# Visits' pieces on four PSUM tiles, batch 1's projections and sorting earlier, and indirect transfers paced by block

## The chip, the cores and the metric

The kernel runs on one core of a Trainium2 chip, as one launch. The metric is the device time of that launch in microseconds (us). All arithmetic is in float32.

## What is computed

The input x is 2 x 256 x 56 x 56: two images, 256 channels, N = 3136 pixels. Two layers follow each other. The first is a non-local block without softmax, so its products can be folded into one 256 x 256 matrix for each image. The second is causal attention over the 3136 pixels as tokens (4 heads of 64), and a mixture of 8 experts of which each token takes its best two.

```python
# layer 0, for each image b; inv, shift are the folded batch norm
f  = einsum('bgdn,bgdm->bgnm', theta(x), phi(x)) / n
y  = einsum('bgnm,bgdm->bgdn', f, g(x))
x  = relu((w_out @ y + b_out) * inv + shift + x)
# layer 1, t = x as tokens, 2 x 3136 x 256
q, k, v = split(layernorm(t) @ W_attn)
t  = t + (softmax(causal(q @ k.T / 8)) @ v) @ W_proj
z  = layernorm(t)
p  = softmax(z @ gate_w + gate_b)          # 8 experts, the two largest kept
t  = t + sum over the two: p[e] * (gelu(z @ W1[e] + b1[e]) @ W2[e] + b2[e])
```

## The kernel before

**Layer 0** (`gram`, `fold`, `apply`) ends at about 92 us with the tokens in `ts[b]`, 128 tokens to a partition block, 25 blocks (`chunk`) to an image; each row has room for 8 gate values and some bookkeeping. Its means and deviations are there too.

**Attention** (`layer1`, `attend`) runs batch 0 and then batch 1. Queries go in 7 blocks of 448 (index i), heads in two pairs (hp), keys in blocks of 128 (j). A step is one (i, hp, j): `scores` makes a score tile (`psc`, two buffers of two PSUM banks each, L721), ACT takes its exponential into `st` (L729; five buffers), DVE multiplies the diagonal blocks by a mask (L731) and adds the tile to a sum (L743); three steps later `values` multiplies by v (L761). Two steps of this order stand in the text as "s" and "y": they alternate on TensorE. When a query block of a head pair has had its last score and TensorE is three steps further, `attend` calls `visit(i, hp)`, and then `sum_rows` (L785).

A **visit** is the place for other matmuls. `ahead` gives its pieces: projections of the next segment's queries and keys (L603), values (L618) and transposes of the normalised tokens (L589), of the next batch too. Every piece takes a PSUM tile from `bank` (pool `pm`, tag "m", two buffers of one bank), which ACT or DVE evicts. A visit also runs output projections.

**The queue.** Work off the main line lies in generators in a queue; each `yield True` is one unit done, `yield False` means that nothing can be done now, and `yield "pe"` that matmuls come next. `pull(n)` runs n units from the first generators that have any. `between` calls it before each attention step (before: `pull(2)` in every other step), `meanwhile` after each block of the expert stage. `products`, called in visits, runs a generator that stands at "pe". For each batch b the generator `tokens` runs in turn:

- `project_out` (L671): pairs of 128-token groups through the output projection, each evicted by an add on DVE (L676), then the layer norm's statistics (`stats`, L177 and L178). With batch 1 each pair is followed by three units.
- `dispatch` (from L1000): the sorting. Softmax of the gate values, the two best experts, ranks by a matmul (L1122), places in the table of slots. Then 25 token groups are normalised (L1355) and scattered twice each by an indirect transfer from GpSimd (L1363) into `x_slots` in DRAM.
- for batch 0, the loads of the experts' first weights and of the first two groups of blocks.

**The expert stage** (`experts`) goes over 102 blocks of 128 slots. Block n runs `hidden` (L1485, sixteen matmuls), the transposes of a later block (L1462) and `outputs` of an earlier one (L1504). The slots come in groups of three blocks, fetched by SP six blocks ahead (L1403, L1408) and for batch 1 added to a second table's rows where both batches share a block (L1439). Blocks from 42 on hold batch 1; `need(1)` in the fetch for block 42, at n = 36, finishes batch 1's scatters if they are not all sent. Weights of a block's expert are copied by DVE (L1473). Results of blocks below 57 are stored to `y_slots`, those from 42 on are scattered to `y_tokens` by GpSimd (L1525).

Once block 56 is written, `finish(0)` joins the queue: for each pair of token groups it gathers the two experts' rows from `y_slots` (L1679, four indirect transfers), DVE adds them with their weights (L1714), TensorE transposes (L1727) and SP stores the result. `finish(1)` does the same for batch 1 from `y_tokens`, with plain loads (L1699).

Inside attention and inside the expert stage the order on every engine is as written out by these loops; nothing reorders it.

Of the kernel before, what the change touches and what calls it, by code (L numbers as in the profile page):

```python
# [10 lines left out]
F32 = mybir.dt.float32  # L11
# [17 lines left out]
def conv_attn_moe_kernel(  # L29
# [52 lines left out]
    P = 128  # L82
    B, C, N = x.shape
# [9 lines left out]
    W = 448  # L93
# [418 lines left out]
    def layer1(nm, general):  # L512

        with ExitStack() as whole:
# [4 lines left out]
            bg = pool(whole, "bg", bufs=2)  # L519
            g1 = pool(whole, "g1", bufs=1)  # L520

            def bank(name, shape=(P, 512)):
                return pm.tile(list(shape), F32, tag="m", name=f"{name}_{nm}")

            def centre_gate(place):
# [135 lines left out]
            def project_out(b, qT, done):  # L661

                for first, m, k in pairs():
                    while done() < (first + m - 1) * P + k:
                        yield False
                    yield "pe"
                    for n in range(first, first + m):
                        o = n * P
                        ps = bank(f"pp_{b}_{n}")
                        for c in range(NH):  # L670
                            nc.tensor.matmul(  # L671
                                ps[:k, : C + E], qT[:, c, o : o + k], wpr[:, c, :],
                                start=(c == 0), stop=(c == NH - 1),
                            )
                        t = ts[b][:k, n, : C + E]
                        nc.vector.tensor_tensor(t, t, ps[:k, : C + E], ALU.add)  # L676
                        if b == 0:
                            nc.sync.dma_start(out=rest_d[:k, n], in_=t[:, :C])
                    stats(b, first, m, k, bg, f"o{nm}{b}")

                    for _ in range(3 if b else 1):
                        yield True

            def attend(
                b, qT, kT, v, fst, fs, psc, py, visit, between, clock, later, finished
# [145 lines left out]
                for n in range(len(steps) + LAG):  # L831
                    if BEHIND < n <= len(steps) + BEHIND and steps[n - 1 - BEHIND][4]:
                        i, hp = steps[n - 1 - BEHIND][:2]
                        visit(i, hp)
                        sum_rows(hp, i)
                    if n < len(steps):
                        i = steps[n][0]
                        between(i, ends[i] - n)
# [165 lines left out]
            def dispatch(b):  # L1004

                t = ts[b]
                tail = chunk(NCH - 1)
                ops = [0]

                def small_piece():  # L1010

# [7 lines left out]

                def op():  # L1020

                    ops[0] += 1
                    for _ in range(0 if b else 1 + ops[0] % 2):
                        yield True

                def small(name, last=E, dt=F32):
# [2 lines left out]
                def wide(ap):  # L1029
# [8 lines left out]
                    small(k, 1).rearrange("p t o -> p (t o)") for k in ("newton_x", "newton_y", "red")  # L1038
                )
                nc.vector.tensor_scalar(x, var, 1e-5, None, ALU.add)  # L1040
                nc.vector.tensor_scalar(
                    y.bitcast(I32), x.bitcast(I32), 1, None, ALU.arith_shift_right
                )
                nc.vector.tensor_scalar(
                    y.bitcast(I32), y.bitcast(I32), -1.0, float(0x5F3759DF), ALU.mult, ALU.add
                )
                yield from small_piece()
                for i in range(4):
                    to = var if i == 3 else y
                    nc.vector.tensor_tensor(z, y, y, ALU.mult)  # L1050
                    nc.vector.tensor_tensor(z, z, x, ALU.mult)
                    nc.vector.tensor_scalar(z, z, -0.5, 1.5, ALU.mult, ALU.add)
                    nc.vector.tensor_tensor(to, y, z, ALU.mult)
                    yield from op()
                    yield from small_piece()
# [294 lines left out]
                for n in range(NCH):  # L1350
                    kk = chunk(n)
                    xr = (scatter_rows[0] if b else bg).tile(
                        [P, width], F32, tag="xr", name=f"xr_{nm}{b}_{n}"
                    )
                    nc.vector.tensor_scalar(  # L1355
                        xr[:kk, :C], t[:kk, n, :C],
                        t[:kk, n, MEAN : MEAN + 1], t[:kk, n, RSTD : RSTD + 1],
                        ALU.subtract, ALU.mult,
                    )
                    if b:  # L1360
                        nc.vector.tensor_copy(xr[:kk, C:], t[:kk, n, C + E - 2 : SLOT + 1])  # L1361
                    for k in range(2):
                        s = nc.gpsimd.indirect_dma_start(  # L1363
                            out=xds[b],
                            out_offset=bass.IndirectOffsetOnAxis(ap=idxs[b][:kk, k, n : n + 1], axis=0),
                            in_=xr[:kk],
                            in_offset=None,
                            bounds_check=xds[b].shape[0] - 1,
                            oob_is_err=False,
                        )  # L1370
                        group = f"x_slots_{nm}{b}"
                        tc.declare_no_dep(s.ins, group=group, reason="different rows")
                        tc.add_to_no_dep_group(group, s.ins)
                        if b or k:
                            yield True
                    if b == 0:
                        yield False
                sent[b] = True

            def experts(w1s, w2s, b2s, ex, es, ps6, between, need, written, settle, decide):  # L1380
# [282 lines left out]
            def finish(b, oy, bufs):  # L1663
# [3 lines left out]
                def fetch(n, m, k):  # L1667
# [8 lines left out]
                    ahead.append((n, m, k, ys, rows))  # L1676
                    for c, y in enumerate(ys):
                        for a in range(m):
                            nc.gpsimd.indirect_dma_start(  # L1679
                                out=y[:k, a],  # L1680
                                out_offset=None,
                                in_=y_slots,
                                in_offset=bass.IndirectOffsetOnAxis(
                                    ap=idxs[b][:k, c, n + a : n + a + 1], axis=0
                                ),
                                bounds_check=MIXED * P - 1,
                                oob_is_err=False,
                            )
                            yield True
# [106 lines left out]
                judged.append(True)  # L1796


            queue, held = deque(), set()

            def advance(g):
                held.discard(g)
# [21 lines left out]

            def products():

                for g in list(queue):
                    if g in held:
                        advance(g)
                        return  # L1830

            projected, placed, ranked, sent = ([False] * B for _ in range(4))
            side, worked, scattered = deque(), [0], []
            first, early_rows, scatter_rows, judged = [], [], [], []
            last_pool, hots = [], []

# [82 lines left out]
            else:  # L1919
                fst = pool(att, "fst", bufs=5)  # L1920
                fs = pool(end, "fs", bufs=2, side="right")
                psc = pool(att, "psc", bufs=2, space=PSUM)
                py = pool(att, "py", bufs=1, space=PSUM)
                projections = [project_qkv(b, qT, kT, v, px) for b in range(B)]
                finished = [[0] * NH for b in range(B)]
# [35 lines left out]
                for piece in keys[2:] + vs(0) + xs(1):  # L1961
                    piece()
                for b in range(B):
                    queue.append(tokens(b, qT, lambda b=b: min(finished[b])))

                    def visit(i, hp):

                        now, then = ahead(b, i, hp)
                        for piece in now:
                            piece()  # L1970
                        for _ in range(2):
                            pull()
                            products()
                        for piece in then:
                            piece()

                    def between(i, left):
                        if b == B - 1 and i == NB - 1 and left < NH * NCH - 2:

                            now = load_w2(left < NCH - 4)  # L1980
# [31 lines left out]
            with ExitStack() as moe:  # L2012
# [35 lines left out]
                    queue.appendleft(finish(1, oy, 3))  # L2048

                def meanwhile():  # L2050
                    sorting = projected[1] and not sent[1]
                    pull(3 if sorting or worked[0] >= MIXED else 2, every=True)
                    if side and next(side[0], None) is None:
                        side.popleft()

                def settle():
                    while queue:
                        pull(every=True)

                def decide():  # L2060
# [181 lines left out]
```

## Time and profile before

| | |
|---|---|
| median of 3 runs | 1320.96 us (1318.52 to 1323.38) |
| the profiled execution | 1319.58 us |
| its span, first to last instruction | 1317.9 us |
| TensorE busy | 1266.8 us |
| DVE, ACT, GpSimd busy | 789.5, 614.4, 343.9 us |
| mean granted TensorE clock | 0.990 |
| layer 0 and the first projections | 0 to 105.3 us, TensorE busy 101.0 |
| attention | 105.3 to 863.1 us, TensorE busy 738.0 |
| expert stage and end | 863.1 to 1317.9 us, TensorE busy 427.7 |

The profile is one execution. The page has the busy time of each engine, the span in 40 slices, and groups of instructions by line. A timeline lists instructions in order, with the idle time ahead of each and what released it in brackets: `[1.08 <-issue]` is 1.08 us of idle time in which the engine waited for nothing that the profile records. Windows give the busy time of every engine in a stretch. Line numbers are those of the kernel before; PE is TensorE, POOL is GpSimd, SP issues transfers.

### The profile page before, as it was taken

How to read it: one execution, taken by the hardware profiler on the slowest of the kernel's cores; microseconds unless marked ns; L12 is line 12 of the kernel's file. 1: busy time of each engine (PE TensorE's matmuls, PEld its weight loads, DVE VectorE, ACT ScalarE, POOL GpSimd, SP SyncE). 2: the span in 40 equal slices, each digit the busy share in tenths (PEclk: the TensorE clock that was granted, in tenths of full speed). 3: DMA queues.
4: the chain of work that ended last, by engine and by line, in shares of the span. 5: the costliest groups of instructions: out<-in, count | busy, mean ns of one | idle time of the engine just before them, and what ended most of it. 6: DMA issues, size and time to landing. Idle time of an engine off the chain costs nothing.

```text
span 1317.9 us, 28546 instructions
## 1 busy us (share of the span) xinstructions
PE 1266.8 (96%) x10809; PEld 821.1 (62%) x10809; DVE 789.5 (60%) x1673; ACT 614.4 (47%) x1235; POOL 343.9 (26%) x319
## 2 busy tenths in 40 slices
PE   8999999999999999999998999999989999899997
PEld 7875545544444445444443444479978899798996
DVE  1673566666777745756876677754843443454554
ACT  0255555556566545565654456542422333244432
POOL 1113220000002223220026630000066212665560
PEclk9999999999999999999999999999989999899999
DMA  9994100000000001000002243322144343555554
GB/s 314 347 348 147 32 16 25 24 17 17 16 10 9 24 1 32 24 9 9 16 28 77 73 140 96 105 72 65 57 142 139 115 113 94 161 177 185 185 169 128
DMA packets 111075, 123.88 MB, mean 94 GB/s; under 512 B 19704, under 2 KB 100841, under 8 KB 110931
## 3 DMA queue, kind: packets, MB, share of 16 engines
q1 hardware_dynamic: 100130, 95.18, 23.6%
q0 software_dynamic: 9840, 25.67, 5.8%
q8 instruction: 89, 1.46, 0.5%
q10 hardware_dynamic: 960, 1.11, 0.2%
q14 instruction: 56, 0.45, 0.1%
HBM read 62.06 MB, written 61.05 MB: 93 GB/s over the span
## 4 chain that ended last, share of the span: by engine, by line
PE 88%; DVE 5%; issue 3%; ACT 2%; DMA 2%; POOL 0%; SPq 0%; another core or an unknown queue 0%; DVEq 0%; POOLq 0%; ACTq 0%
PE sc_f L721 19%; PE yp_f L761 19%; PE ht_f L1485 13%; PE yp_f L1504 13%; PE qk_f L603 7%; PE v_f L618 4%; PE cp L410 3%; PE pp_f L671 3%; PE tp_f L1462 2%; PE gram L317 2%; DVE acc_f L743 1%; PE sp_f L785 1%; ACT st_f L729 1%; PE yo_f L1727 1%; DMA out_dram<-ot_f 1%
## 5 line engine op out<-in xcount | busy, mean ns | idle before, releaser
L743 DVE TENSOR_TENSOR acc_f<-acc_f,st_f 128x896 f32<-128x896 f32 (+5 forms) x372 | 376.0, 1011 | 147.3 <-ACT st_f L729 128.3
L729 ACT ACTIVATE st_f<-sc_f 128x896 f32<-128x896 f32 (+5 forms) x400 | 330.3, 838 | 215.0 <-PE sc_f L721 193.1
L761 PE MATMUL yp_f<-st_f,v_f 64*64 64x448 f32 (+6 forms) x3184 | 337.9, 500 | 4.6 <-DVE st_f L731 3.1
L721 PE MATMUL sc_f<-qT_f,kT_f 64*64 64x448 f32 (+6 forms) x3184 | 336.3, 499 | 5.6 <-ACT st_f L729 3.8
L1494 ACT ACTIVATE g_f<-ht_f,b1b 128x128 f32<-128x128 f32 x408 | 116.9, 372 | 253.5 <-PE ht_f L1485 120.7
L721 PEld LDWEIGHTS sc_f<-qT_f,kT_f 64*64 64x64 f32 x3184 | 118.1, 133 | 160.9 <-issue 139.9
L761 PEld LDWEIGHTS yp_f<-st_f,v_f 64*64 64x64 f32 x3184 | 117.0, 133 | 158.2 <-issue 128.7
L1485 PE MATMUL ht_f<-xT_f,w_f 128*128 128x128 f32 x1632 | 205.3, 278 | 10.2 <-issue 7.3
L1485 PEld LDWEIGHTS ht_f<-xT_f,w_f 128*128 128x128 f32 x1632 | 199.8, 194 | 17.7 <-issue 12.8
L773 POOL TENSOR_TENSOR qT_f<-acc_f 128x448 f32<-128x448 f32 x28 | 31.9, 1140 | 492.6 <-ACT acc_f L772 492.6
L1363 POOL DMA_INDIRECT x_slots<-xr_f,idx x100 | 110.1, 1101 | 154.9 <-DVE xr_f L1361 104.9
L1473 DVE COPY w_f<-w1s_f 128x1024 f32 x102 | 72.4, 712 | 86.6 <-PE ht_f L1485 31.2
L574 POOL TENSOR_SCALAR xn_f<-t 128x256 f32<-128x256 f32 (+1 forms) x50 | 81.9, 1645 | 158.7 <-PE xp_f L589 69.7
L1525 POOL DMA_INDIRECT y_tokens<-ys_f,to_f x57 | 58.2, 1021 | 125.8 <-DVE ys_f L1514 101.4
L603 PE MATMUL qk_f<-px_f,wat 128*128 128x512 f32 (+2 forms) x224 | 89.9, 556 | 0.6 <-ACT px_f L595 0.6
L1514 DVE TENSOR_TENSOR ys_f<-yp_f,kT_f 128x128 f32<-128x128 f32 x102 | 29.5, 290 | 96.5 <-PE yp_f L1504 69.3
L603 PEld LDWEIGHTS qk_f<-px_f,wat 128*128 128x128 f32 x224 | 42.2, 197 | 45.8 <-issue 41.0
L1504 PE MATMUL yp_f<-px_f,g_f 128*128 x204 | 62.2, 386 | 1.4 <-PE tp_f L1462 1.3
L1504 PE MATMUL yp_f<-kT_f,g_f 128*128 x204 | 61.9, 385 | 0.7 <-issue 0.7
L1504 PE MATMUL yp_f<-w2s_f,g_f 128*128 x204 | 62.2, 386 | 0.0
L1504 PE MATMUL yp_f<-v_f,g_f 128*128 x204 | 62.1, 386 | 0.0
L731 DVE TENSOR_TENSOR st_f<-st_f,keep 128x256 f32<-128x256 f32 (+1 forms) x112 | 45.1, 402 | 28.0 <-ACT st_f L729 26.4
(285 smaller groups left out, 1221.8 us busy)
## 6 DMA issues: line engine op xcount, KB each, us to landing
x_slots<-fill SPq DMA_DIRECT2D x1, 8190.0 KB
xb_f<-x_slots SPq DMA_DIRECT2D x60, 130.0 KB
x_slots<-fill SPq DMA_DIRECT2D x1, 7296.0 KB
y_slots<-ys_f SPq DMA_DIRECT2D x57, 128.0 KB
kept<-t SPq DMA_DIRECT2D x2, 3200.0 KB
x<-in_x_dram SPq DMA_DIRECT2D x14, 448.0 KB
rb_f<-inverses SPq DMA_DIRECT2D x56, 112.0 KB
y_f<-y_tokens SPq DMA_DIRECT2D x23, 256.0 KB
```

The lines of the kernel that those rows point to most:

```text
L574: nc.gpsimd.tensor_scalar(xn[:k, a], ts[b][:k, n + a, :C], ts[b][:k, n + a, MEAN : MEAN + 1], ts[b][:k, n + a, RSTD : RSTD + 1], ALU.subtr ...
L603: nc.tensor.matmul(ps[:, :w], wat[:, c, d0 : d0 + P], px[:, s % 2, c, :w], start=(c == 0), stop=(c == NH - 1),)
L721: nc.tensor.matmul(ps[h : h + HS, a, c0:W], kT[hp][rows, j * P + h : j * P + h + HS], qT[rows, hp, q0 + c0 : q0 + W], start=True, stop=True,)
L729: nc.scalar.activation(st[:k, :, c0:], ps[:k, :, c0:W], AF.Exp, scale=SCALE)
L743: nc.vector.tensor_tensor(acc[:k, :, c0:], acc[:k, :, c0:], st[:k, :, c0:], ALU.add)
L761: nc.tensor.matmul(yp[a * HS : (a + 1) * HS, h // HS, c0:W], v[hp][h : h + HS, j, a, :HS], st[h : h + HS, a, c0:], start=first, stop=bool( ...
L1363: s = nc.gpsimd.indirect_dma_start(out=xds[b], out_offset=bass.IndirectOffsetOnAxis(ap=idxs[b][:kk, k, n : n + 1], axis=0), in_=xr[:kk], i ...
L1473: nc.vector.tensor_copy(w, w1s[:, :, bass.ds(e, 1), :].rearrange("p c e h -> p c (e h)"))
L1485: nc.tensor.matmul(ht[:, k, :], w[:, c, k * P : (k + 1) * P], xT[:, c, :], start=(c == 0), stop=(c == NH - 1),)
L1494: nc.scalar.activation(g[:, k, :], ht[:, k, :], AF.Gelu, bias=b1bs[b][:, k, i : i + 1])
L1504: nc.tensor.matmul(yp[:, :C], g[:, k, :], w2s[k][:, bass.ds(e, 1), :].rearrange("p e d -> p (e d)"), start=(k == 0), stop=(k == KH - 1),)
L1525: s = nc.gpsimd.indirect_dma_start(out=y_tokens, out_offset=bass.IndirectOffsetOnAxis(ap=to[:, n % GB : n % GB + 1], axis=0), in_=ys, in_o ...
```

## The change

- In a visit, `bank` counts its calls (`ring`) and gives tiles 1 and 2 from `pm` and tiles 3 and 4 from the score pool `psc`, and so on in turn. `visit` sets the count and clears it at its end, ahead of `sum_rows`.
- `project_out` no longer takes statistics on the spot. It puts a generator `closer` in the queue that does one group's statistics a unit: for batch 0 at the front, for batch 1 ahead of the queue's last entry. No unit follows a pair of batch 0 any more, and one follows a pair of batch 1. Only when all statistics of the batch are taken does it go on.
- `products` walks the batches, not the queue, and advances a batch's projections until it has done one pair. A visit calls it twice, now without a `pull` before each.
- `between` pulls one unit each step in place of two in every other step, and none in the cut (diagonal) steps of the first query block.
- `dispatch` for batch 0 yields after each operation, the Newton steps' too, where before it yielded once and twice in turn, and the four operations of a Newton step counted as one. In its scatter loop a unit follows each pair of transfers, and a second one that was a `yield False`.
- `finish(0)` issues one or two gathers a block in turn (`gathered`, `turn`). While batch 1's scatters go on `meanwhile` pulls two or three units in turn, in place of three; from block 57 on four in place of three.

```diff
             def bank(name, shape=(P, 512)):
+                turn = ring[0] % 4 if ring else 0
+                if turn > 1:
+                    ring[0] += 1
+                    flat = score_banks[0].tile([P, 2, 512], F32, tag="sc", name=f"{name}_{nm}")[:, 0]
+                    ...
+                    return flat[:, : shape[1]]
+                if ring:
+                    ring[0] += 1
                 return pm.tile(list(shape), F32, tag="m", name=f"{name}_{nm}")
...
-                    stats(b, first, m, k, bg, f"o{nm}{b}")
-
-                    for _ in range(3 if b else 1):
+                    if b == 0:
+                        queue.appendleft(closer(b, first, m, k))
+                    else:
+                        queue.insert(len(queue) - 1, closer(b, first, m, k))
                         yield True
+                while unclosed[b]:
+                    yield False
+
+            unclosed = [NCH] * B
+
+            def closer(b, first, m, k):
+
+                for n in range(first, first + m):
+                    stats(b, n, 1, k, bg, f"o{nm}{b}")
+                    unclosed[b] -= 1
+                    yield True
...
                 def op():
-                    ops[0] += 1
-                    for _ in range(0 if b else 1 + ops[0] % 2):
+                    if b == 0:
                         yield True
...
                     if b == 0:
-                        yield False
+                        yield True
                 sent[b] = True
...
                         for a in range(m):
+                            while gathered[0] == 1 + turn[0] % 2:
+                                yield False
+                            gathered[0] += 1
                             nc.gpsimd.indirect_dma_start(
...
             def products():
-                for g in list(queue):
-                    if g in held:
+                for b, g in enumerate(batches):
+                    if projected[b]:
+                        continue
+                    r = "pe" if g in held else advance(g)
+                    while r is True and not projected[b]:
+                        r = advance(g)
+                    if r == "pe":
                         advance(g)
                         return
...
                         now, then = ahead(b, i, hp)
+                        ring.append(0)
                         for piece in now:
                             piece()
                         for _ in range(2):
-                            pull()
                             products()
                         for piece in then:
                             piece()
+                        ring.clear()
-                    def between(i, left):
+                    def between(i, left, cut):
...
-                        if tick[0] % 2:
-                            pull(2)
+                        if not cut or i:
+                            pull()
...
                 def meanwhile():
-                    sorting = projected[1] and not sent[1]
-                    pull(3 if sorting or worked[0] >= MIXED else 2, every=True)
+                    gathered[0] = 0
+                    turn[0] += 1
+                    if placed[1] and not sent[1]:
+                        pull(2 + turn[0] % 2, every=True)
+                    else:
+                        pull(
+                            4 if worked[0] >= MIXED else 3 if projected[1] and not sent[1] else 2, every=True
+                        )
```

More of the change, by code (lines that the diff above doesn't have):

```diff
@@ L520, in layer1 @@
             g1 = pool(whole, "g1", bufs=1)
+            ring, score_banks = [], []
             def bank(name, shape=(P, 512)):
+                turn = ring[0] % 4 if ring else 0
+                if turn > 1:
+                    ring[0] += 1
+                    flat = score_banks[0].tile([P, 2, 512], F32, tag="sc", name=f"{name}_{nm}")[:, 0]
+                    if shape[2:]:
+                        return flat[:, : shape[1] * shape[2]].rearrange("p (a w) -> p a w", a=shape[1])
+                    return flat[:, : shape[1]]
+                if ring:
+                    ring[0] += 1
                 return pm.tile(list(shape), F32, tag="m", name=f"{name}_{nm}")
@@ L837, in attend @@
                         i = steps[n][0]
-                        between(i, ends[i] - n)
+                        between(i, ends[i] - n, (steps[n][2] + 1) * P > i * W + 1)
                     late = n >= LAG and steps[n - LAG][3]
@@ L1007, in dispatch @@
                 tail = chunk(NCH - 1)
-                ops = [0]
                 def small_piece():
@@ L1040, in dispatch @@
                 nc.vector.tensor_scalar(x, var, 1e-5, None, ALU.add)
+                yield from op()
                 nc.vector.tensor_scalar(
@@ L1043, in dispatch @@
                 )
+                yield from op()
                 nc.vector.tensor_scalar(
@@ L1046, in dispatch @@
                 )
+                yield from op()
                 yield from small_piece()
@@ L1050, in dispatch @@
                     nc.vector.tensor_tensor(z, y, y, ALU.mult)
+                    yield from op()
                     nc.vector.tensor_tensor(z, z, x, ALU.mult)
+                    yield from op()
                     nc.vector.tensor_scalar(z, z, -0.5, 1.5, ALU.mult, ALU.add)
+                    yield from op()
                     nc.vector.tensor_tensor(to, y, z, ALU.mult)
@@ L1796, in judge @@
                 judged.append(True)
-            queue, held = deque(), set()
+            queue, held, batches = deque(), set(), []
             def advance(g):
@@ L1833, in layer1 @@
             side, worked, scattered = deque(), [0], []
+            gathered, turn = [0], [0]
             first, early_rows, scatter_rows, judged = [], [], [], []
@@ L1922, in layer1 @@
                 psc = pool(att, "psc", bufs=2, space=PSUM)
+                score_banks.append(psc)
                 py = pool(att, "py", bufs=1, space=PSUM)
@@ L1963, in layer1 @@
                 for b in range(B):
-                    queue.append(tokens(b, qT, lambda b=b: min(finished[b])))
+                    batches.append(tokens(b, qT, lambda b=b: min(finished[b])))
+                    queue.append(batches[b])
                     def visit(i, hp):
                         now, then = ahead(b, i, hp)
+                        ring.append(0)
                         for piece in now:
@@ L2057, in settle @@
                     while queue:
+                        gathered[0] = 0
                         pull(every=True)
```

## The prediction

> **What bounds the kernel now.** I read the page first: busy shares, slices, instruction queue.
>
> ```profile
> PE 1266.8 (96%) x10809; PEld 821.1 (62%) x10809; DVE 789.5 (60%) x1673; ACT 614.4 (47%) x1235; POOL 343.9 (26%) x319
> ...
> PE   8999999999999999999998999999989999899997
> ...
> PEclk9999999999999999999999999999989999899999
> ...
> q8 instruction: 89, 1.46, 0.5%
> ```
>
> TensorE has work 96% of the span of 1317.9 us, so no edit here gains more than its idle time plus what it loses at a lowered clock. Idle is 51.1 us. Windows over the stages split it: 4.3 us before attention, 19.8 in attention (105.3 to 863.1), 18.9 from 863.1 until TensorE's last matmul, 8.2 behind that while the last output lands. The first and the last part are out of the change's reach; 38.7 us are within it. Then who ended TensorE's waits:
>
> ```profile
> PE ht_f L1485 <- issue: 7.3, 13, 1.1
> PE tp_f L1462 <- issue: 3.4, 4, 2.0
> PE yp_f L761 <- DVE st_f L731: 3.1, 7, 1.1
> ...
> PE xp_f L589 <- DVE t L676: 2.2, 6, 1.2
> PE sp_f L785 <- ACT kT_f L611: 1.8, 7, 0.4
> ```
>
> The columns are total us, times, longest. Two families: small waits for PSUM evictions around the visits, and "issue", where a matmul waited for nothing recorded. For the second I opened TensorE's timeline:
>
> ```profile
> 1133.51 1.05 PE L1485 MATMUL ht_f<-xT_f,w_f 128*128 128x128 f32 x8
> 1134.86 0.36 PE L1485 MATMUL ht_f<-xT_f,w_f 128*128 128x128 f32 x1 [0.30 <-issue]
> 1136.30 0.27 PE L1485 MATMUL ht_f<-xT_f,w_f 128*128 128x128 f32 x1 [1.08 <-issue]
> 1137.02 0.27 PE L1485 MATMUL ht_f<-xT_f,w_f 128*128 128x128 f32 x1 [0.45 <-issue]
> ...
> 1142.02 1.01 PE L1504 MATMUL yp_f<-px_f,g_f 128*128 x2 [0.85 <-PE tp_f L1462]
> ```
>
> Matmuls that run eight in 1.05 us suddenly come one by one, and at 1142 a pair takes 1.01 us instead of 0.59. The windows of that stretch give engines' busy time, clock, and DMA share and rate (last three columns):
>
> ```profile
> 1125.00:1130.00 5.00, 5.00 (x35) 4.66 (x33) 0.97 (x3) 1.63 (x7) 3.98 (x4) 1.00 0.79 249
> ...
> 1135.00:1140.00 5.00, 2.38 (x8) 1.64 (x9) 0.38 (x2) 0.00 (x0) 3.78 (x5) 0.73 0.50 161
> 1140.00:1145.00 5.00, 3.73 (x11) 2.74 (x10) 1.50 (x4) 2.60 (x10) 2.20 (x3) 0.50 0.20 60
> ```
>
> GpSimd (fifth) is 76 to 80% busy in the stretch's first two windows shown, issuing indirect transfers one behind the other. By the steady lengths in TensorE's timeline (hidden 1.78, transpose 0.22, output product 1.73: 3.73 us a block) I priced each such place, idle and lowered clock together: 974.0 to 987.2 holds 5.46 us of work, 7.7 lost; 1004 to 1009.8, 3.8; 1019.1 to 1024.7, 1.9; 1133.5 to 1148.6, 9.2. Sum 22.6 us. All lie while scatters of batch 1 or gathers of batch 0 are queued back to back. A fifth, 1040.1 to 1049.7, loses 3.9 and is another thing: DVE's timeline has the add xb+xo (L1439) starting only at 1042.99, released by the landing of xo, and SP issued that block's loads at 1037.5, just after the last scatter (POOL, 1034.89).
>
> **What the Trainium skill says.** (1) *Runtime: NRT & Kernel Launch*, Instruction fetch mechanics: instructions are refilled in 16 KiB blocks over the sequencer's own DMA queue, and crossing a block is mostly hidden. The page's q8 agrees on size: 1.46 MB in 89 packets is 16.4 KB each. (2) *DMA: Bandwidth & Descriptors*, Issuing engines are not separate DMA queues: all transfers interleave on the same 16 engines. Together they make late instruction fetches behind dense indirect traffic the likeliest reading of "issue". The trace shows the coincidence, not the cause. (3) *TensorE: Matmul & The Clock Gate*, What's actually happening: about 3.4 us of little work halve the clock. The trace agrees: 0.50 in 1140 to 1145. (4) *PSUM — Partial Sum Buffer*: eight banks, an output in one. The four tiles of a visit are two of one bank and two score pairs of two; with the two of the y tile, all eight are in use before and after.
>
> **The change, part by part.** The instruction order of both kernels has the same TensorE instructions; only places move, so TensorE's work is priced at nothing.
>
> *Four PSUM tiles in a visit.* Before, a visit's pieces and the sums behind them wait for the tile used two pieces ago. The timeline puts on this: sums (L785) 4.0 us, transposes (L589) 2.4, projections (L671) 0.6, and of the 2.7 at 705.7 (values, L618) about 0.9, since there the second score tile frees at 705.3. That is 7.9. With four tiles each wait looks back twice as far, 1.8 us or more of matmuls against copies of 0.44 (L627) and adds of 0.43 (L676), so I expect them gone. But in the shortest blocks TensorE next waits for ACT's copy of the y tile (0.58 at 121.35, 0.63 at 498.53), which follows the same copies: 1.4 comes back. Gain 6.5; bounds 3 and 8.
>
> The other side: the first score after a visit needs a score tile that a piece has used. In a visit of four value and four projection pieces the seventh piece has it; behind its matmuls come one projection (0.9), a transpose (0.6), the sums (0.6), a values step (0.75): 2.8 us against one 0.43 add. I charge 0.5, bounds 0 and 32 (below, the slower rival).
>
> *Statistics apart, sorting one operation a step.* Before, a visit puts two pairs' adds and statistics on DVE at once: 4 x 0.43 + 4 x (0.41 + 0.18) = 4.1 us, and batch 0's sorting two to four operations every other step; waits for the mask product (L731) cost 3.1 us. After, each step of 1.5 us gets one. Half comes back: gain 1.5, bounds 0 and 2.5. Against it, twenty statistics of batch 1 now lie on twenty successive steps of the last query block: DVE 1.01 + 0.59 = 1.60 against 1.50, a lag of some 2 us by the end, on top of 1.7 for the visit's adds. Five score buffers in SBUF hold about three steps. Cost 1, bounds 0 and 4.
>
> *Batch 1's projections earlier.* By TensorE's order eight groups of 128 tokens (0.9 us each) go from the expert stage into visits, and the ten before them to earlier visits: neutral on TensorE. At the seam TensorE waits 2.3 us for the weight copy (L1473), which stood behind two adds and two statistics on DVE; DVE comes free about 2.3 us sooner, TensorE 2.0: gain 0.4, bounds 0 and 1.
>
> *Sorting sooner.* By DVE's order (weight copies count blocks) batch 1's scatters begin around block 15 instead of 22 and end around 34 instead of 37. The first batch 1 fetch stands at block 36, so its landing no longer follows the scatters: the 3.9 us at 1040 go. Behind it on SP are the y_slots stores, which move up too. Bounds 2 and 4.
>
> *Transfers paced.* Scatters fall from 50 in 15.5 blocks to 50 in 19.5. At 1.29 us each (0.98 busy, 0.30 between, POOL's timeline), GpSimd's need goes from 4.1 us a block, over the 3.73 that a block lasts, to 3.3. Gathers begin with 2,1,2,1,2,1 a block instead of 3,3,2,2,2,0; with one y_tokens scatter each and 1.33 apiece the first six blocks need 3.3 instead of 4.0 us each. No backlog is left in either stretch. Yet the total is the same, and after these first blocks the gathers now keep a higher rate (1.35 a block against 1.1), where the old kernel had no such stall. In attention batch 0's scatters keep their pace (25 tiles in 48 steps against 44), and I leave the stalls there (742 to 748 and ACT's at 702 to 766, 9 us) as they are. Nothing shows the threshold: of 22.6 us I take 8, bounds -8 (density spread over 58 blocks adds stalls) and 22.6.
>
> New waits: the gather's generator yields, it does not wait; nothing on POOL queues behind it but y_tokens scatters, which come sooner. Transposes waiting for the final adds (L1727, 2.5 us) I leave.
>
> Sum: 6.5 - 0.5 + 1.5 - 1 + 0.4 + 3.9 + 8 = 18.8. The profiled execution took 1319.58 (span plus 1.7), giving 1300.8; the median stands 1.4 above it: **1302**.
>
> **Rivals.**
> - *The supply stalls stay as long, elsewhere.* The trace has them in attention's scatters too, at two transfers every 3 us, so unsaturated GpSimd is no protection. 1302 + 8 = **1310**.
> - *They vanish.* For it: 1146 to 1284 has 79.7 us of GpSimd in 138 and not one. 1302 - 14.6 = **1287**.
> - *The gains are taken back.* ACT evicts in order, so visit waits return at the next values step (gain 2 instead of 6.5), and the longer dense phase adds as much as it saves: 1302 + 4.5 + 8 = 1314.5, with 2 to 4 us from the DVE lag **1317**, no change.
> - *Slower: scores wait for projections.* If DVE runs more than 2.8 us late at visits, the first score after each of the 27 visits with pieces waits for L676. At 1.2 us each: 1302 + 32 = **1334**. It decides from about 1.0 us a visit. Against it: in slices of 33 us DVE is busy for 27.0 at most in attention.
> - That the change doesn't do what it says is excluded by the order.
>
> **Chances.** Forecast 0.46, stalls stay 0.21, vanish 0.13, taken back 0.13, slower 0.07. Half a per cent, 6.6 us, is about what a measurement can tell from no change. Faster is the first three, 0.80; same 0.13; slower 0.07. The range leaves out the slower case, the upper part of taken back and the lower edge of vanish: 1288 to 1316; its lower end rests on the unknown supply term.
>
> **What would show it.** Right: L785, L589 and L671 lose their idle; no wait of some 2 us at the first batch 1 transposes; issue waits of the expert stage down by a third and fewer stretches at clock 0.5. Wrong: a score (L721) waiting for DVE L676 right after visits; L731 waits growing near the end of attention; issue waits spread over 1150 to 1280.

## The result and the profile after

In runs beside each other the changed kernel took 1300.76 us (median of 6, 1298.13 to 1305.54), the kernel before 1320.1 us (6 runs): ratio 0.9856, 95% interval 0.9835 to 0.9877. The forecast was 1302 us. The profiled execution of the changed kernel took 1305.54 us (span 1303.7), the slowest of the six; its span is 14.2 us under that of before, while the medians differ by 19.3. What follows explains the 14.2.

The page's lines of the changed kernel:

```profile
PE 1259.5 (97%) x10809; PEld 820.1 (63%) x10809; DVE 783.4 (60%) x1673; ACT 612.0 (47%) x1235; POOL 346.7 (27%) x319
...
PE   8999999999999999999999899979999999999997
...
PEclk9999999999999999999999999999999999999999
...
q8 instruction: 89, 1.46, 0.5%
```

The dips of the last third are fewer and the clock's eights have gone, but there is a new 7 at the slice of 847 to 880 us. The waits of TensorE (total us, times, longest) name it:

```profile
PE pp_f L682 <- DVE qT_f L840: 6.7, 1, 6.7
PE sc_f L744 <- ACT st_f L752: 5.1, 8, 1.3
PE qk_f L614 <- ACT st_f L752: 4.2, 1, 4.2
...
PE ht_f L1512 <- issue: 2.2, 4, 0.9
PE yo_f L1757 <- issue: 2.1, 1, 2.1
PE yp_f L1531 <- issue: 1.9, 4, 0.7
PE yp_f L784 <- DVE st_f L754: 1.8, 5, 0.8
PE yp_f L784 <- ACT acc_f L795: 1.8, 3, 0.6
PE tp_f L1489 <- issue: 1.4, 3, 0.7
PE sp_f L808 <- DVE acc_f L766: 1.2, 1, 1.2
```

Line numbers are those of the changed kernel: L682 was L671, L808 was L785, L600 was L589, L1512 was L1485, L1489 was L1462, L754 was L731, L1757 was L1727, L1531 was L1504, L614 was L603, L744 and L752 were L721 and L729. L600's waits are gone from the list, L808's fell from 4.0 to 2.1 us in all. Issue waits of hidden products fell from 7.3 to 2.2. Those of transposes fell from 3.4 to 1.4, but 2.0 of the 3.4 was the wait at 1044 for the first fetch of batch 1, which the profile lists as "issue" too; and those of output products rose from 0.7 to 1.9. At the top stands one single wait of 6.7 us that did not exist. The 4.2 us are new as well: a projection of a visit, at 744.8, waits for a score tile that ACT's exponential still holds.

The issue stretch beside the gathers, where the kernel before had one at 1133.5 to 1148.6, in TensorE's timeline and in the windows (columns: length, then PE, PEld, DVE, ACT and POOL busy, clock, DMA share and rate):

```profile
1122.22 1.88 PE L1512 MATMUL ht_f<-xT_f,w_f 128*128 128x128 f32 x12
1125.05 0.39 PE L1512 MATMUL ht_f<-xT_f,w_f 128*128 128x128 f32 x2 [0.94 <-issue]
1125.77 0.27 PE L1512 MATMUL ht_f<-xT_f,w_f 128*128 128x128 f32 x1 [0.33 <-issue]
...
1127.33 1.02 PE L1531 MATMUL yp_f<-kT_f,g_f 128*128 x2
```

```profile
1120.00:1125.00 5.00, 3.97 (x26) 3.58 (x26) 0.89 (x5) 0.00 (x0) 3.79 (x4) 1.00 0.56 180
1125.00:1130.00 5.00, 4.19 (x15) 3.24 (x15) 2.71 (x6) 2.71 (x10) 2.07 (x3) 0.74 0.54 160
```

Same signs, about half as long: twelve products in a run, then ones and twos 0.72 us apart, then pairs of 1.0 us at half clock.

To sum what was lost whatever its name, I took the time between the starts of each two successive matmuls and subtracted the median of that kind of pair (the same two lines and tiles) in the same trace. "The sum by pairs" below means this:

```
us lost on TensorE              before   changed   gain
862.9 to 900   seam               2.7      9.3     -6.6
900 to 1030    scatters          13.7      6.0      7.7
1030 to 1060   first fetch        3.9     -0.1      4.0
1060 to 1160   gathers begin      8.9      5.3      3.6
1160 to 1260   final adds         3.1      0.7      2.4
1260 to end    last outputs       0.4      4.2     -3.8
```

That is 7.3 us. In attention the same group of scores starts 7.07 us sooner (577.66 before, 570.59 after, both timelines). By the end of attention only 0.2 to 0.3 us of this lead is left, because eight projection groups (32 matmuls of 0.22, 7.1 us) stand there which the expert stage no longer has. So attention gained about 7.4 us. 7.4 and 7.3, with 0.5 less tail, are 15.2 against 14.2 in the spans: the method is good to 1 us.

### The profile page after: what moved, and what is told of

It reads as the page before. It is cut to its first block, busy times and chain, and to the rows that moved or that the text cites. A ratio compares the mean times of both kernels' runs of the same rounds, so it can differ in the third digit from the quotient of the medians.

```text
span 1303.7 us, 28517 instructions
## 1 busy us (share of the span) xinstructions
PE 1259.5 (97%) x10809; PEld 820.1 (63%) x10809; DVE 783.4 (60%) x1673; ACT 612.0 (47%) x1235; POOL 346.7 (27%) x319
## 4 chain that ended last, share of the span: by engine, by line
PE 92%; DVE 2%; ACT 2%; issue 1%; DMA 1%; another core or an unknown queue 1%; SPq 0%; DVEq 0%; ACTq 0%
PE sc_f L744 20%; PE yp_f L784 20%; PE ht_f L1512 14%; PE yp_f L1531 13%; PE qk_f L614 7%; PE v_f L629 4%; PE pp_f L682 4%; PE cp L410 3%; PE gram L317 2%; PE tp_f L1489 2%; PE sp_f L808 1%; ACT st_f L752 1%; DVE acc_f L766 1%; PE xp_f L600 1%; PE yo_f L1757 1%
## 5 line engine op out<-in xcount | busy, mean ns | idle before, releaser
L766 DVE TENSOR_TENSOR acc_f<-acc_f,st_f 128x896 f32<-128x896 f32 (+5 forms) x372 | 373.7, 1004 | 136.5 <-ACT st_f L752 123.6
L752 ACT ACTIVATE st_f<-sc_f 128x896 f32<-128x896 f32 (+5 forms) x400 | 330.0, 838 | 217.3 <-PE sc_f L744 186.7
L744 PE MATMUL sc_f<-qT_f,kT_f 64*64 64x448 f32 (+6 forms) x3184 | 336.2, 499 | 5.6 <-ACT st_f L752 5.1
L744 PEld LDWEIGHTS sc_f<-qT_f,kT_f 64*64 64x64 f32 x3184 | 118.2, 133 | 160.6 <-issue 138.1
L1512 PE MATMUL ht_f<-xT_f,w_f 128*128 128x128 f32 x1632 | 203.7, 278 | 3.1 <-issue 2.2
L1512 PEld LDWEIGHTS ht_f<-xT_f,w_f 128*128 128x128 f32 x1632 | 199.7, 194 | 9.4 <-issue 3.3
L585 POOL TENSOR_SCALAR xn_f<-t 128x256 f32<-128x256 f32 (+1 forms) x50 | 84.9, 1704 | 157.7 <-PE xp_f L600 68.6
L614 PE MATMUL qk_f<-px_f,wat 128*128 128x512 f32 (+2 forms) x224 | 88.9, 549 | 4.8 <-ACT st_f L752 4.2
L614 PEld LDWEIGHTS qk_f<-px_f,wat 128*128 128x128 f32 x224 | 40.8, 191 | 50.2 <-issue 41.0
L1531 PE MATMUL yp_f<-w2s_f,g_f 128*128 x204 | 61.3, 381 | 1.2 <-issue 1.2
L754 DVE TENSOR_TENSOR st_f<-st_f,keep 128x256 f32<-128x256 f32 (+1 forms) x112 | 45.1, 402 | 28.8 <-ACT st_f L752 26.8
L1531 PE MATMUL yp_f<-kT_f,g_f 128*128 x204 | 61.5, 384 | 0.7 <-issue 0.7
L1531 PE MATMUL yp_f<-px_f,g_f 128*128 x204 | 61.4, 383 | 0.0
L1531 PE MATMUL yp_f<-v_f,g_f 128*128 x204 | 61.1, 381 | 0.0
```

The costliest lines, as they stand in the source:

```text
L585: nc.gpsimd.tensor_scalar(xn[:k, a], ts[b][:k, n + a, :C], ts[b][:k, n + a, MEAN : MEAN + 1], ts[b][:k, n + a, RSTD : RSTD + 1], ALU.subtr ...
L614: nc.tensor.matmul(ps[:, :w], wat[:, c, d0 : d0 + P], px[:, s % 2, c, :w], start=(c == 0), stop=(c == NH - 1),)
L744: nc.tensor.matmul(ps[h : h + HS, a, c0:W], kT[hp][rows, j * P + h : j * P + h + HS], qT[rows, hp, q0 + c0 : q0 + W], start=True, stop=True,)
L752: nc.scalar.activation(st[:k, :, c0:], ps[:k, :, c0:W], AF.Exp, scale=SCALE)
L766: nc.vector.tensor_tensor(acc[:k, :, c0:], acc[:k, :, c0:], st[:k, :, c0:], ALU.add)
L1512: nc.tensor.matmul(ht[:, k, :], w[:, c, k * P : (k + 1) * P], xT[:, c, :], start=(c == 0), stop=(c == NH - 1),)
```

## What the experiments showed

The runs fell on three chips, on which the kernel before took 1285.0, 1314.5 and 1321.3 us. So times are compared within one group of runs only, and by the ratio to the kernel before in the same group. Times in the first four forecasts, such as 1307 us, are counted from the group of the result; only their differences can be compared.

**First chip (before: 1285.0 us).** The changed kernel itself was not run on this chip, only variants of it. Visits back on two tiles:

```diff
                         now, then = ahead(b, i, hp)
-                        ring.append(0)
```

> The changed kernel with the visits back on two PSUM tiles; all else as changed. Theory: the waits for evictions around visits come back, as the sum priced them: 6.5 us, so 1307 us. Rival: the waits fell because each step now gives DVE one operation, and the two extra tiles are worth little: 1302 us, and the sums' and transposes' waits stay under 1 us in the trace.

Measured: 1285.03 us, ratio 1.0001 (0.9992 to 1.001). The waits are back:

```profile
PE pp_f L682 <- DVE t L687: 1.9, 2, 1.4
...
PE sp_f L808 <- ACT kT_f L622: 1.2, 5, 0.2
PE sp_f L808 <- ACT v_f L638: 1.2, 4, 0.3
```

Against the bunched variant below, which has the four tiles, the scores fall 8.1 us behind over attention, and the time is 9.7 us longer. Without the tiles the rest of the change, with its losses at the seam and at the last output, is worth nothing on this chip. The rival fell: the sums (L808) alone wait 4.2 us again.

Projections held back:

```diff
-                        for _ in range(2 * 2 if wait > 4 else 0):
+                        for _ in range(2 * 3 if wait > 4 else 2 * 2 if wait > 2 else 0):
                             yield True
```

> The changed kernel with the last five projections of batch 1 held back by about three more expert blocks, and the reciprocal of the last sums by two. Theory: TensorE's wait of 6.7 us for the last scaled values (L840) behind the end of attention, and the half clock after it (2.5 us), both go, since the round trip of the sums through DRAM (some 14 us) is covered again: 1301 - 9 = 1292 us. Rival: sorting and scatters of batch 1 start three blocks (11 us) later, and what they lose there or at the first fetch of batch 1 gives it back: 1299 to 1302 us.

Measured: 1269.39 us, ratio 0.9878 (0.9859 to 0.9898). The seam in windows, held back first, then the bunched variant, which has the changed kernel's seam:

```profile
855.00:860.00 5.00, 5.00 (x41) 4.85 (x40) 1.59 (x3) 3.53 (x13) 0.00 (x0) 1.00 0.25 68
860.00:865.00 5.00, 5.00 (x34) 4.61 (x33) 2.05 (x6) 1.41 (x5) 0.00 (x0) 1.00 0.27 91
```

```profile
855.00:860.00 5.00, 0.00 (x0) 0.00 (x0) 1.42 (x4) 0.00 (x0) 0.00 (x0) 0.93 0.41 124
860.00:865.00 5.00, 4.99 (x21) 4.79 (x22) 1.53 (x5) 0.30 (x2) 0.00 (x0) 0.50 0.00 1
```

An empty window and one at clock 0.50 have become two full ones. Six us of the nine show in the medians (1275.32 to 1269.39), 7.2 by the last matmul of the two traces; sorting that begins later costs nothing visible. The two kernels differ in the bunching too, but by the sum by pairs the scatters lose 0.1 to 0.2 us in both.

Old pacing (this edit, and no limit on gathers), and bunched scatters:

```diff
-                    gathered[0] = 0
-                    turn[0] += 1
-                    if placed[1] and not sent[1]:
-                        pull(2 + turn[0] % 2, every=True)
...
+                    sorting = projected[1] and not sent[1]
+                    pull(3 if sorting or worked[0] >= MIXED else 2, every=True)
```

```diff
-                        pull(2 + turn[0] % 2, every=True)
+                        pull((4, 4, 2, 0)[turn[0] % 4], every=True)
```

> The changed kernel with the old pacing of the expert stage: three scatters or three gathers a block, no limit on gathers. Theory (density): the issue waits of both stretches grow back to the old kernel's: some 10 us, so 1311 us, with runs of twelve or more transfers back to back on GpSimd. Rival: it was the sooner sorting that moved the stalls, pacing has no part: 1301 us.

> The changed kernel with the same ten scatters of batch 1 in each four blocks, but bunched 4, 4, 2, 0 instead of 2, 3, 2, 3. Theory (unbroken runs of about eight transfers or more on GpSimd stall the other engines' issue; pauses cure it): runs of ten, each with a stall of some 2 us, five of them: 1301 + 8 = 1309 us. Rival (only the mean rate counts): 1301 us. Second rival (the pause after each ten is as good as many short ones): 1297 us.

Measured: old pacing 1273.64 us, ratio 0.9913 (0.9897 to 0.9929); bunched 1275.32 us, 0.9926 (0.991 to 0.9942). Neither forecast of added waits held. The windows of the old pacing's scatters on this chip say why:

```profile
920.00:940.00 20.00, 20.00 (x139) 18.27 (x138) 11.73 (x51) 7.01 (x25) 15.68 (x15) 1.00 0.48 154
940.00:960.00 20.00, 20.00 (x141) 18.62 (x140) 10.70 (x36) 7.01 (x25) 15.43 (x16) 1.00 0.51 173
```

GpSimd (15.4 to 15.7 of 20 us, all 50 scatters back to back with only 0.30 us between) could not be denser, and TensorE loses nothing. Issue waits beside the transfers do not exist in this chip's four traces, with any pacing. Old pacing lies 1.7 us under the bunched variant, within the intervals; the wait of 2.1 us for the last output of batch 0 is absent from its trace.

**Second chip (before: 1314.5 us).** Two kernels unchanged; the pacing alone (the edits of `meanwhile` and of the gathers, on the kernel before); and both edits above together (held back, old pacing):

> The kernel before, unchanged, for a trace on the chip of these runs. In the first four runs the kernel before took 1285 us, 35 less than in the runs of the result, and the traces of the changed kernel had no issue waits in their transfer stretches. Theory: the issue waits depend on the chip or the hour, not on the kernel alone; if this chip shows 1285 us, the trace has under 2 us of issue waits on TensorE and otherwise the old waits at visits (about 10 us) and at the seam (2.3). Rival: they are there as before (some 11 us by name, 22 with what they slow).

> The changed kernel, unchanged, timed beside the others on one chip. Theory: where no issue waits are seen, the pacing and the sooner scatters have nothing to save; visits (6.5), the first fetch (up to 3.9) and statistics (0.5) against the seam (9 lost, 2.3 saved) and the last output (4 lost) remain: the old time less 1 to 8 us, ratio 0.994 to 0.999. Rival: the same ratio as in the result, 0.986.

> The kernel before with the new pacing of the expert stage alone. Theory: without issue waits to save it gains nothing, and the gathers' limit costs up to 4 us at the last batch 0 output: ratio 1.000 to 1.003. If the chip has issue waits: half of them go, ratio 0.993. Rival: the pacing is a gain of its own, 0.993 on any chip.

> The changed kernel with the last five projections held back, and the old pacing of the expert stage. Theory: the two gains of the first four runs add up (seam: about 8 us; no gather limit before the last batch 0 output: about 4 us): ratio 0.985 beside a 1285 us kernel before, 1265 us. Rival: they overlap, and it is no better than holding alone, 0.988. If the chip has issue waits, the old pacing brings back some 10 us of them, and holding alone is better.

Measured: before, a single run, 1313.98 us; changed 1300.79 us, ratio 0.99 (0.9872 to 0.9927), that is 13.7 us, which is neither of its two forecasts; pacing alone 1310.32 us, 0.9968 (0.9952 to 0.9985); held back with old pacing 1304.38 us, 0.9933 (0.991 to 0.9956). This chip has the issue waits; the kernel before:

```profile
PE ht_f L1485 <- issue: 6.4, 14, 1.1
PE yp_f L1504 <- issue: 3.8, 10, 0.8
```

So here pacing is worth 4.2 us by itself (2.0 to 6.3). Its trace shows why it isn't more. By the sum by pairs it loses 13.0 us less than the kernel before beside the transfers: 8.0 against 15.8 in the scatters' stretch (940 to 1030) and 2.8 against 8.0 in the gathers' (1060 to 1160). But from 1030 to 1060 it loses 9.6 us where the kernel before loses 2.3, and at the last output 2.2 more than it. TensorE reaches block 36 seven us sooner (1012.1 against 1019.4), while the last scatter ends no sooner (1030.8 against 1028.7). So TensorE waits for the first fetch of batch 1, with the clock at 0.50 from 1035 to 1040:

```profile
1038.96 0.66 PE L1462 MATMUL tp_f<-ident,xb_f 128*128 128x128 f32 x2 [3.95 <-issue]
```

The changed kernel, whose sorting begins sooner, loses nothing there; beside the transfers it loses 6.6 and 4.9 us, 12.3 less than the kernel before. In these traces, one of each kernel, the pacing accounts for the whole fall of the issue waits, and the earlier sorting lets TensorE keep it.

Without the pacing the mended seam shows no gain: the median is 3.6 us above the changed kernel's, though the intervals overlap. In its trace the old pacing brings back 9.7 us beside the transfers (14.5 and 6.7 lost against 6.6 and 4.9), the ten that were forecast and more than the seam gives. Its windows of scatters, with the same pacing as in the windows of the first chip:

```profile
935.00:955.00 20.00, 16.39 (x104) 14.21 (x102) 8.68 (x38) 4.21 (x15) 12.95 (x13) 1.00 0.41 137
...
995.00:1015.00 20.00, 16.93 (x97) 14.60 (x96) 5.96 (x21) 5.50 (x20) 7.40 (x7) 0.83 0.29 88
```

Held beside the first chip's: there 20.00 us busy with GpSimd at 15.7, here 16.4 and 16.9 with GpSimd lower. By the sum by pairs the scatters of the first chip lost 0.1 to 0.2 us in all four variants.

**Third chip (before: 1321.3 us).** The changed kernel unchanged; held back with two gathers in each block; this with scatters bunched; and the four tiles alone on the kernel before (the new `bank`, and `ring` set and cleared in `visit`).

```diff
-                            while gathered[0] == 1 + turn[0] % 2:
+                            while gathered[0] == 2:
```

> The changed kernel, unchanged, beside the three others. So far: ratio 0.986 and 0.990 on chips that show issue waits; on the one that shows none the bunched variant, which differs only in what makes issue waits, had 0.993. Theory: 0.986 to 0.990 with issue waits in its trace, 0.991 to 0.994 without.

> The changed kernel with the last five projections held back and a limit of two gathers in every block instead of one and two in turn; scatters paced as changed. Theory: the seam's 9 us go, and the last output of batch 0 comes soon enough that TensorE's wait of 2.1 us for it and the half clock after it go too (3.8), while the pacing that matters stays: 12 us under the changed kernel beside it. Rival: two gathers a block with a y_tokens scatter are again unbroken runs, and on a chip with issue waits they take 4 us back: 8 us under.

> As the kernel with two gathers a block, but the ten scatters of each four blocks bunched 4, 4, 2, 0. Theory (length of unbroken runs makes issue waits): on a chip with issue waits, five runs of ten cost 2 us each more: 8 to 10 us over the kernel with two gathers. Rival (mean rate only): within 2 us. On a chip without issue waits: within 1 us, and nothing is told apart.

> The kernel before with the four PSUM tiles in turn alone. Theory: 6.5 to 8 us, as the sum had it and as the changed kernel without them lost, ratio 0.994. Rival: together with two pairs' adds and statistics in one visit the tiles gain half of it, 3 us, ratio 0.998, since DVE is the later one then.

Measured: changed 1302.4 us, ratio 0.986 (0.9839 to 0.988); two gathers 1301.49 us, 0.9849 (0.9827 to 0.987); bunched 1304.16 us, 0.9867 (0.9848 to 0.9886); four tiles alone 1310.8 us, 0.9925 (0.9907 to 0.9944), that is 9.9 us (7.4 to 12.3).

Two gathers a block gave no measurable gain: the forecast of 12 us fell. In its trace the seam is mended and the last batch 0 output waits 1.2 us in place of 2.1, and that execution took 1293.85 us, but it was the fastest of six; one other took 1295, four took 1301 to 1305. Even in that trace the gathers' stretch (1060 to 1160) lost 9.5 us by the sum by pairs, the changed kernel's 5.4 beside it: the rival's 4 us. What took the rest in the other executions no trace shows. The edit also changed two things at once; holding back alone was not run on a chip with issue waits. In the traces the seam itself is mended on every chip: from 3 us ahead of the first hidden product to 37 behind it, the four held-back variants lose 1.3 us each, all others that have the change's projections 8.1 to 9.9.

Bunching: 11.5 us lost in the scatters' stretch against 4.7. But the intervals of the times overlap, and the edit hardly made longer runs: the longest unbroken run of scatters has 10 transfers in the bunched trace and 12 in the other. So what length of runs does stays unsettled.

## Why the prediction was right, and where it was not

The time and the sign came true, partly because errors cancelled.

*Four PSUM tiles: right, and larger.* Priced 6.5 us net of 1.4 that would come back and 0.5 for scores. Measured 8.1 (first chip, by traces) and 9.9 (alone, by time). Of the priced 7.9 us about 0.9 is left in the result's list (sums waiting for ACT's copies), and hardly anything came back: waits for ACT's copy of the y tile (L795) are 1.2 us on the first chip with the tiles and without; in the result's trace they grew from 1.2 to 1.8. The slower rival, scores waiting for projections, has no entry in any list: no L744 <- DVE t L687. The other direction has one that the prediction did not name, the 4.2 us of L614 <- L752, amid the stalls of attention's scatters. In the traces of the same kernel on the other two chips it is absent, a variant on the third has it again; whether the tiles cost anything there was not separated.

*Statistics apart: right in kind.* Waits for the mask product fell from 3.1 to 1.8 us (1.3, priced 1.5). The lag by the end of attention is the 1.2 us by which the last sums wait for DVE (L808 <- L766), priced 1.

*Projections earlier: wrong, the failed step.* It said "neutral on TensorE" for the moved groups and gained 0.4 at the seam. By the sum by pairs the seam lost 6.6 us more instead. The changed kernel's timeline:

```profile
868.40 1.50 PE L682 MATMUL pp_f<-wpr,qT_f 128*128 128x264 f32 x6
...
870.25 0.20 DVE L828 RECIPROCAL back_f<-sums 128x7 f32<-128x7 f32 x1 [5.94 <-DMA sums<-sums]
...
875.89 0.63 DVE L840 TENSOR_TENSOR qT_f<-qT_f,rb_f 128x448 f32<-128x448 f32 x1 [3.72 <-DMA rb_f<-inverses]
...
876.57 1.25 PE L682 MATMUL pp_f<-wpr,qT_f 128*128 128x264 f32 x2 [6.67 <-DVE qT_f L840]
```

Four of the five groups left need the last query block's scaled values: its row sums go to DRAM and back, are inverted, and go to DRAM and back once more, from ACT's copy at 862.1 to the scaling at 875.9. In the kernel before the scaling came at the same time, but the pair of groups that first needs it started 21.8 us later:

```profile
876.28 0.62 DVE L817 TENSOR_TENSOR qT_f<-qT_f,rb_f 128x448 f32<-128x448 f32 x1 [3.41 <-DMA rb_f<-inverses]
```

```profile
898.06 1.94 PE L671 MATMUL pp_f<-wpr,qT_f 128*128 128x264 f32 x8
```

The eight groups were cover. I knew from the order which groups move and which stay, priced the moved ones by their own length, and did not ask what the remaining ones then wait for. After the wait comes half clock. The Trainium skill (*TensorE: Matmul & The Clock Gate*, What's actually happening) says that TensorE goes back to half its clock after an idle window of about 3.4 us, and the trace agrees: here 6.7 idle us are followed by 5 us at 0.50. Holding the five groups back removes both.

*First fetch: right.* The 3.9 us at 1040 are gone (4.0 by the sum). In the trace of the kernel before on the second chip that wait was not there, so it is not a gain in every run; with the pacing alone it was there and longer (3.95 us).

*Pacing: direction right, term too small, mechanism not shown.* Of 22.6 us, which the sum by pairs confirms (13.7 and 8.9), half went, 11.3, where I took 8. On the second chip the pacing alone took as much from this as the whole change; its 4.2 us of time are what the first fetch and the last output left of that. The prediction explained the gain by a lower need of GpSimd and no backlog. The traces don't bear this out: the fifty scatters took 80.0 us before and 81.1 after, with GpSimd busy for 52.5 and 52.2 of them, and the longest unbroken run was 12 and then 10 (on the second chip 12, and 14 with pacing alone). They are spread over 19.2 blocks in place of 17.0, but each block is shorter, since less of it is lost. What in the pacing shortens the waits stays open.

*Left unchanged: wrong in two places that nearly cancel.* The final adds' waits fell by 2.4, which I had left alone. The limit on gathers costs 3.8 at the last output of batch 0 (2.1 of them the wait, which is in every trace with this limit and in none without): its add stands behind three one-hot steps, a weight copy and two adds of DVE.

```profile
1259.10 1.36 DVE L1578 TENSOR_SCALAR hot_f<-hot_f,xb_f,w_f 128x448 f32<-128x448 f32 x3
...
1261.38 0.98 DVE L1744 SCALAR_TENSOR_TENSOR res_f<-y_f,wt,res_f 64x256 f32<-64x256 f32 x2
...
1262.46 0.31 PE L1757 MATMUL yo_f<-ident,res_f 64*128 64x64 f32 x2 [2.09 <-issue]
```

Against the forecast's sum of 18.8: -7.0 at the seam, -3.8 and 2.4 just told, 3.3 more of issue waits, 0.9 more in attention, 0.1 at the fetch, 0.5 of tail: 15.2. That the median came within 1.3 us of the forecast is luck on top of this: the profiled execution stood 4.7 us above the 1300.8 forecast for it; the median, 4.8 us under that execution, came 1.2 under its forecast.

*The cause of the issue waits: my reading is not supported.* The Trainium skill (*Runtime: NRT & Kernel Launch*, Instruction fetch mechanics) has instructions refilled in blocks of 16 KiB, 256 instructions each, and the crossing mostly hidden; the prediction took late refills for likeliest. In the trace of before, a packet of q8 comes about every 253 TensorE instructions, weight loads counted, as this says. But waits without a recorded cause begin 19 to 173 instructions after the last packet, with no fixed place between two. The packets are 89 in every run; they take 1.16 us in the mean there and 1.13 in the run without tiles on the first chip, where such waits don't exist. Nor is a long unbroken run of transfers enough: 50 in a row are harmless there. Why some groups of runs have the waits stays open.

## What to carry to other kernels

Before moving work forward, ask what it stood in front of: if what stays behind waits for a chain through DRAM, the moved work was its cover, and its absence costs the chain's rest and the half clock after it. A gain in one stretch can turn into a wait in the next: pacing alone brought TensorE to the first fetch before the scatters had ended. Don't count on a wait that the profile can't name before a second chip shows it, and compare within one group of runs. When a sum comes true, check its terms: here 10.8 us that did not come and 7.2 that nobody forecast were hidden in it.

## What the runs showed of the hardware

The same kernel took 1285.0 us on one chip and 1314 to 1321 on two others. Each chip was used in one group of runs only, so chip and hour are not told apart. The difference to 1320.1, 35.1 us, is by these traces mostly issue waits beside indirect transfers: 22.6 us in the expert stage, and about 7 in attention's scatters (690 to 775 us: 36.3 us by the sum by pairs against 29.4 on the first chip, where the run without tiles shows 0.3 us of idle time). While such waits last, TensorE's products start some 0.72 us apart, in ones and twos, instead of each 0.11 us (16 in 1.78). The kernel before left no trace on the first chip; the four variants of the changed kernel stand for it. A gain that comes from avoiding such waits is seen only where they occur: pacing alone gave 0.9968 on a chip that has them; on the chip without them, bunched and old pacing made no difference that the intervals separate.
